# A sparse graph transformer on one core: ranks inverted by one-hot products on TensorE, lists gathered per tile, first attention from the eighth query tile

## The chip, the cores and the metric

The kernel runs on one core of a Trainium2 chip. Its engines are named as in the profile: PE (TensorE, matrix products), DVE (VectorE), ACT (ScalarE), POOL (GpSimd) and SP, which only issues transfers. The metric is the device time of one execution in microseconds; the runs of the kernel before took 1945.95, 1947.1 and 1948.37 us, so the median is 1947.1 us.

## The reference

Two layers of a graph transformer over 2708 tokens of 512 features, with 8 heads of 64. A token attends only to the tokens that `adj` joins it with (itself included); the adjacency is sparse.

```python
mask = adj.astype(jnp.float32) + jnp.eye(n, dtype=jnp.float32)
q = (h @ Wq.T + bq).reshape(n, N_HEADS, D_K)
k = (h @ Wk.T + bk).reshape(n, N_HEADS, D_K)
v = (h @ Wv.T + bv).reshape(n, N_HEADS, D_K)
scores = jnp.einsum('nhd,mhd->hnm', q, k) / jnp.sqrt(jnp.float32(D_K))
scores = jnp.where(mask[None, :, :] == 0, jnp.float32(-1000000000.0), scores)
attn = jax.nn.softmax(scores, axis=-1)
ctx = jnp.einsum('hnm,mhd->nhd', attn, v).reshape(n, D_MODEL)
attn_out = ctx @ Wo.T + bo
h1 = _layer_norm(h + attn_out, ln1_g, ln1_b)
ff = jax.nn.relu(h1 @ W1.T + b1) @ W2.T + b2
h2 = _layer_norm(h1 + ff, ln2_g, ln2_b)
```

The second layer does the same with the first layer's output and its own weights. All is float32; the hidden layer of the feed-forward has 2048 columns.

## The kernel before

**Tiles.** The 2708 tokens are 22 tiles (NT) of 128, the last with 20 tokens. Keys and values of a layer are written to memory as one row of 1024 numbers per token (kv_d), queries as rows of 512 (q_d). Attention never forms the full score matrix: for each token there is a list of at most 24 neighbours, and rows of kv_d are gathered by list position, 128 tokens at a time, by indirect transfers that POOL issues.

**Ranks.** Tokens have between 1 and 22 neighbours. They are put in order of that count, longest list first, and attention works on tiles of ranked tokens. Tile g then needs only `CAPS[g]` gathers: 22 for tile 0, 7 for tiles 16 to 18, 6 for tile 19, 5 for tile 20. The work goes in blocks of two ranked tiles: (20, 19), (18, 17), (7, 9), (6, 10) and so on; `order` is that list laid flat.

**Stage 1, `first` (0 to about 157 us).** For each of 22 tiles PE makes k and v; DVE adds the bias to k (L879), ACT copies v (L881) and writes the pair to kv_d. Beside it `lists` turns rows of `adj` into lists: POOL adds the diagonal, ACT makes codes of position and flag (L681), DVE takes the greatest by groups of eight (L684 to L691). With the last tile `counted` finds each token's count, the place of each count in the order (`before`, `hot`), and the records `rec`: 24 list entries, the token's own number in column 24, and padding to 32 numbers (128 bytes).

**Stage 2, `first_queries` (about 162 to 285 us).** For each of 22 tiles PE makes q; DVE scales it and adds the bias (L929); SP writes pairs of tiles to q_d. At t = 1 `ranked` makes each token's rank (two PE products, L763 and L770, and four DVE operations), and POOL scatters the 22 tiles of records to their rank in `rec_d` (L789), then loads them back in ranked order in three parts (L801, L808); the token numbers go to `ident_i`, the lists to `idx`, and a penalty for unused places to `minus` (`listed`). `own_rows` gathers the x rows of the first ranked tiles, `own_query` makes their queries directly, since q_d isn't complete yet. At t = OWN (13) those of tiles 20 and 19 are made and attention begins; at each later t `advance` lets attention emit more of its steps.

**Attention, `attend`.** The lists are cut into chunks of at most two gathered rows per token (1024 or 2048 numbers a partition). A chunk's steps are the product with the query (L1055) and its sum by head (L1061) on DVE; one step later the exponentials (L1074) and the weighting (L1081) on ACT and the sums on DVE (L1087, L1094); two steps later, for a tile's last chunk, the tile's sums and the reciprocal (L1102 to L1117); three steps later ACT's division to `cx` (L1125). `advance(c)` adds c to a credit, at most 1.5, and emits steps while it is positive and fewer than two tiles are done and not taken. A chunk of two rows costs 1. Gathers are issued three chunks ahead (EARLY), into five buffers (KVB).

**After attention.** `attended` transposes cx on PE (L1191), multiplies by Wo (o, L576), adds x, and norms on DVE with a power on POOL (L1181). `feed_forward` makes 16 slices f of the hidden layer (pf, L1383; ACT's relu to ft, L1394) and, three slices later, the second product (a, L1356). During the feed-forward of one block attention for the next is emitted; `through(k+1)` at f = 10 (11 for the first block) makes it complete.

**What sets the order.** PE, ACT and SP take the order of the source (`manual_schedule`). POOL does so in stages 1 and 2 and in layer 0's feed-forward, DVE in `first_queries`; elsewhere a scheduler orders DVE and POOL, and it moves an independent DVE operation into the gap between two dependent ones. An engine runs its instructions strictly in the built order, so one that waits holds all that stand behind it. Buffers come from pools: q takes turns in three PSUM banks "g" (even t) and three "f" (odd t), and k, v, transposes and own queries share them.

Of the kernel before, what the change touches and what calls it, by code (L numbers as in the profile page):

```python
# [43 lines left out]
XB, XBS = 256, 11  # L44
LEAD = 1.3
QT = 6
OWN = 13
EARLY = 3
FIRST = 5
PACE = (0.62, 0.72)  # L50


# [420 lines left out]
def by_edges(ctx: ExitStack, tc: tile.TileContext, x, xT, adj, layers, out, good):  # L473
# [130 lines left out]
    def lists_of(pa):  # L604
# [7 lines left out]
        for code in codes:  # L612
# [13 lines left out]
        nc.gpsimd.memset(top[:, NT - 1, :], 0.0)  # L626
        rec = pa.tile([P, NT, 32], F32, tag="rec", name="rec", bufs=1)
        nc.gpsimd.memset(rec, 0.0)
        nc.gpsimd.iota(
            rec[:, :, LIST : LIST + 1],  # L630
            [[P, NT], [1, 1]],
            base=0,
            channel_multiplier=1,
            allow_small_or_imprecise_dtypes=True,
        )
        by = pa.tile([P, LIST], F32, tag="by", name="by", bufs=1)
        nc.gpsimd.iota(
            by,
# [15 lines left out]
        new = dn.tile([P, NC, 2 * P], F32, tag="hT", name="new", bufs=1)  # L654
        new = new.rearrange("p c t -> p (c t)")[:, : NT * 32]
        new = new.rearrange("p (g c) -> p g c", c=32)
        nc.gpsimd.memset(new, 0.0)
        nc.gpsimd.dma_start(
            out=rec_d[: (NT - 1) * P, :].rearrange("(g p) c -> p g c", p=P),
            in_=new[:, : NT - 1, :],  # L660
        )
        nc.gpsimd.dma_start(out=rec_d[(NT - 1) * P :, :], in_=new[:LW, NT - 1, :])

        full = []

# [90 lines left out]
        def ranked(hot, before, half):  # L756

            at = pa.tile([P, NT], F32, tag="at", name="at", bufs=1)
            for h in range(2):
                ts = slice(h * half, (h + 1) * half)  # L760
                pr = ps_a.tile([P, DM], F32, tag=f"a{h}", name="pr")
                w = half * LIST
                nc.tensor.matmul(  # L763
                    pr[:, :w],
                    tri,
                    hot[:, ts, :].rearrange("p t e -> p (t e)"),
                    start=True,
                    stop=False,
                )
                nc.tensor.matmul(  # L770
                    pr[:, :w],
                    ones,
                    before[:, ts, :].rearrange("p t e -> p (t e)"),
                    start=False,
                    stop=True,
                )
                nc.vector.tensor_tensor(
                    hot[:, ts, :].rearrange("p t e -> p (t e)"),
                    hot[:, ts, :].rearrange("p t e -> p (t e)"),
                    pr[:, :w],  # L780
                    ALU.mult,
                )
                nc.vector.tensor_reduce(at[:, ts], hot[:, ts, :], AX.X, ALU.add)
            ranks = pa.tile([P, NT], I32, tag="ranks", name="ranks", bufs=1)
            nc.vector.tensor_copy(ranks, at)
            moved = []
            for t in range(NT):
                r = size(t)
                move = nc.gpsimd.indirect_dma_start(  # L789
                    out=rec_d[:, :],  # L790
                    out_offset=bass.IndirectOffsetOnAxis(ap=ranks[:r, t : t + 1], axis=0),
                    in_=rec[:r, t, :],
                    in_offset=None,
                    bounds_check=N - 1,
                    oob_is_err=False,
                )
                tc.declare_no_dep(move.ins, group="moved", reason="no two tokens have one rank")
                tc.add_to_no_dep_group("moved", move.ins)
                moved.append(move)
            def back(a, b):  # L800
                load = nc.gpsimd.dma_start(  # L801
                    out=new[:, a:b, :],
                    in_=rec_d[a * P : b * P, :].rearrange("(g p) c -> p g c", p=P),
                )
                return load

            first, last = NT - FIRST, NT - 1
            rest = nc.gpsimd.dma_start(out=new[:LW, last, :], in_=rec_d[last * P :, :])  # L808
            for load in (rest, back(first, last), back(0, first)):
                for move in moved:  # L810
                    tc.add_manual_dep(
                        load.ins,
                        move.ins.name,
                        mybir.DependencyInfo(
                            mybir.DependencyClass.Sync, mybir.DependencyReason.DATA
                        ),
                        reason="every list is in its place",
                    )
            nc.gpsimd.tensor_copy(ident_i[:, first:], new[:, first:, LIST])

        def listed(start):

            ts = slice(NT - FIRST, NT) if start else slice(0, NT - FIRST)
            if not start:
                nc.gpsimd.tensor_copy(ident_i[:, ts], new[:, ts, LIST])
            some = new[:, ts, :LIST]
            nc.vector.tensor_scalar(idx[:, ts, :], some, 1.0, 1.0, ALU.max, ALU.subtract)
            nc.vector.tensor_scalar(minus[:, ts, :], some, 0.0, NEG, ALU.is_equal, ALU.mult)

        return lists, counted, ranked, listed  # L830

    def first(w, meanwhile):

# [33 lines left out]
        bk = next(turning)  # L867
        wv = matrix(w, "Wv", "wv")
        pa = tc.tile_pool(name="pa", bufs=2)
        lists, counted, ranked, listed = lists_of(pa.__enter__())  # L870
        done, before = 0, None
        for t in range(NT):
            r = size(t)
            xs = tokens(t, 0)
            kv = wts.tile([P, 2 * DM], F32, tag=f"w2_{5 + t % 3}", name="kvs")
            k = project(xs, r, wk, "k")
# [4 lines left out]
            nc.scalar.copy(kv[:r, DM:], v[:r])  # L881
            if before:
                nc.scalar.dma_start(**before)
            if t == NT - 1:
                counts = counted()
            plus_rest(kv[:r, :DM], k, r)
            plus_rest(kv[:r, DM:], v, r)
            before = dict(out=kv_d[0][t * P : t * P + r, :], in_=kv[:r])
# [9 lines left out]
                bq = next(turning)  # L898
                finish(turning)
        nc.scalar.dma_start(**before)  # L900
        return bq, wq, counts, ranked, listed, pa, tokens

    def first_queries(bq, wq, counts, ranked, listed, pa, tokens, meanwhile):

        nonlocal at
        made = []

        def written():
# [9 lines left out]
        for t in range(NT):  # L918
# [2 lines left out]
                written()  # L921
            q = project(tokens(t, 1), r, wq, "q", other=t % 2 > 0)
            if t == 1:
                ranked(*counts)
                xrs = [own_rows(g) for g in order[:3]]
            if t % 2 == 0:
                qs = wts.tile([P, 2, DM], F32, tag=f"w2_{5 + t // 2 % 3}", name="qs")
                made.append((t, qs))
            nc.vector.scalar_tensor_tensor(  # L929
                qs[:r, t % 2], q[:r], DK**-0.5, bq[:r], ALU.mult, ALU.add  # L930
            )
            plus_rest(qs[:r, t % 2], q, r, DK**-0.5)
            if t == OWN - 1:
                listed(True)
                pa.__exit__(None, None, None)
                at = ctx.enter_context(tc.tile_pool(name="at", bufs=2))
                for g in order[:3]:
# [6 lines left out]
                    own_query(g, zT, to[g], bq, wq)  # L944
                    advance(0.5)
            if t == OWN + 1:
                listed(False)
                xr = own_rows(order[3])
            if t == OWN + 4:
                own_query(order[2], zTs[2], to[order[2]], bq, wq)  # L950
                zT = turned_own(order[3], xr)
            meanwhile(t)
            if t == NT - 1:
                g = order[3]
                own[g] = at.tile([P, DM], F32, tag="q", name="q", bufs=QB)
                own_query(g, zT, own[g], bq, wq)
# [584 lines left out]
    def beside_queries(t):  # L1541
# [5 lines left out]
            now.load_w1(len(now.w1), nc.scalar)  # L1547
            now.load_w2(len(now.w2), nc.scalar)
        if t > OWN:
            advance(1.0 if t < NT - 3 else 0.6)  # L1550
        if t == NT - 3:
            through(0)
            early[0] = now.attended(blocks[0], got)
            next(early[0])
        if t == NT - 2:
            for _ in blocks[0]:
                next(early[0])

# [176 lines left out]
```

## Time and profile before

| what | value |
| --- | --- |
| median of three runs | 1947.1 us |
| the profiled execution | 1944.02 us, its span 1942.3 us |
| mean granted clock of PE | 0.982 |
| DMA in the span | 366.92 MB, 189 GB/s on average |
| PE busy, 100 to 150 us / 200 to 250 us | 48.52 / 47.46 us |
| PE busy, 350 to 400 us / 900 to 1000 us | 45.74 / 100.00 us |

A line of a timeline has the start in us from the span's start, the duration in us, the engine, the source line, the operation, the tile written and those read, shapes, the count of merged instructions, and in brackets the idle time before it with what ended it. A PE product of float32 counts twice: its 4 parts stand as x8.

The gathers of keys are the costliest group of POOL, and the key products of DVE:

```profile
L1018 POOL DMA_INDIRECT kv<-kv_d,idx x420 | 544.5, 1296 | 461.8 <-DVE acc L1094 272.4
L1055 DVE TENSOR_TENSOR kv<-kv,q 128x1024 f32<-128x1024 f32 (+3 forms) x222 | 254.3, 1157 | 171.1 <-DMA kv<-kv_d,idx 139.9
```

After the bar stand busy time and the mean of one in ns, then the idle time before such an instruction and what ended most of it.

### The profile page before, as it was taken

The numbers are of one execution on the slowest core, as the hardware profiler recorded it, in microseconds if no ns is written. First come the engines' busy times: TensorE is split into PE (matmuls) and PEld (weight loads), VectorE is DVE, ScalarE is ACT, GpSimd is POOL, SyncE is SP. The second block draws the span as 40 slices with busy tenths as digits, with TensorE's granted clock in tenths as the row PEclk, the third lists the DMA queues.
The fourth block names the chain that finished last, engine by engine and source line by source line (L and its number), as shares of the span: only waits on it lengthen the run. The fifth ranks groups of instructions, "written<-read, shape, count | busy, mean of one in ns | idle before, by whom it ended". The sixth has DMA issues, their size and how long they took to land.

```text
span 1942.3 us, 20878 instructions
## 1 busy us (share of the span) xinstructions
PE 1859.4 (96%) x6162; PEld 1098.8 (57%) x6162; DVE 1321.4 (68%) x2172; ACT 934.0 (48%) x3219; POOL 804.6 (41%) x710
## 2 busy tenths in 40 slices
PE   8998968999999999999999997999999999999997
PEld 4443426556666565665666553566666665666664
DVE  5885467758658686785840337697977998878422
ACT  4560135545536555474452113556465766655511
POOL 3013525435536555463510114354555776546101
PEclk9999978999999999999999999999999999999999
DMA  9998747556645665554501368665665766544000
GB/s 330 345 319 297 260 151 269 181 176 198 199 159 181 215 201 175 188 185 151 170 17 65 110 237 325 215 220 186 216 213 165 262 215 235 184 154 151 17 1 19
DMA packets 131486, 366.92 MB, mean 189 GB/s; under 512 B 16669, under 2 KB 37005, under 8 KB 128655
## 3 DMA queue, kind: packets, MB, share of 16 engines
q0 software_dynamic: 69120, 246.35, 38.0%
q1 hardware_dynamic: 53332, 99.66, 14.9%
q10 hardware_dynamic: 8910, 19.48, 2.7%
q8 instruction: 50, 0.82, 0.2%
q14 instruction: 74, 0.60, 0.1%
HBM read 314.62 MB, written 50.83 MB: 188 GB/s over the span
## 4 chain that ended last, share of the span: by engine, by line
PE 48%; issue 3%; DVE 3%; DMA 1%; POOL 1%; ACT 1%; POOLq 0%; SPq 0%; DVEq 0%
PE pf L1383 19%; PE a L1356 18%; PE o L576 4%; PE q L576 2%; PE k L576 1%; PE v L576 1%; PE tp L1191 1%; DVE kv L1055 1%; POOL kv L1018 1%; DVE sc L1061 1%; DMA kv<-kv_d,idx 1%; PE a L1371 1%; DMA q<-q_d 0%; DVE acc L1094 0%; POOL rd L1181 0%
## 5 line engine op out<-in xcount | busy, mean ns | idle before, releaser
L1018 POOL DMA_INDIRECT kv<-kv_d,idx x420 | 544.5, 1296 | 461.8 <-DVE acc L1094 272.4
L1383 PE MATMUL pf<-hT,w 128*128 128x256 f32 (+1 forms) x2816 | 637.2, 374 | 6.7 <-ACT ft L1394 5.2
L1383 PEld LDWEIGHTS pf<-hT,w 128*128 128x128 f32 x2816 | 521.4, 192 | 181.8 <-issue 104.1
L1356 PE MATMUL a<-w,ft 128*128 128x512 f32 x1312 | 615.0, 595 | 6.1 <-ACT ft L1394 3.6
L1055 DVE TENSOR_TENSOR kv<-kv,q 128x1024 f32<-128x1024 f32 (+3 forms) x222 | 254.3, 1157 | 171.1 <-DMA kv<-kv_d,idx 139.9
L1394 ACT ACTIVATE ft<-pf,b 128x256 f32<-128x256 f32 (+1 forms) x336 | 153.8, 463 | 432.7 <-PE pf L1383 428.8
L1356 PEld LDWEIGHTS a<-w,ft 128*128 128x128 f32 x1312 | 247.8, 191 | 196.5 <-issue 169.3
L1081 ACT ACTIVATE kv<-kv,p 128x64 f32<-128x64 f32 x1232 | 311.0, 334 | 5.0
L1061 DVE TENSOR_REDUCE sc<-kv 128x16 f32<-128x1024 f32 (+3 forms) x222 | 253.7, 1152 | 1.5
L1094 DVE TENSOR_TENSOR acc<-acc,kv 128x1024 f32<-128x1024 f32 (+2 forms) x178 | 203.9, 1145 | 17.5 <-ACT kv L1081 15.5
L1181 POOL TENSOR_TENSOR rd<-va,mhalf 128x1 f32<-128x1 f32 (+1 forms) x88 | 90.0, 1023 | 273.5 <-DVE va L1179 271.9
L576 PE MATMUL o<-wo,cT 128*128 128x512 f32 x336 | 149.7, 598 | 0.5 <-ACT cT L1196 0.5
L1087 DVE TENSOR_TENSOR kv<-kv,p 128x512 f32<-128x512 f32 (+1 forms) x178 | 121.2, 681 | 36.1 <-ACT p L1074 36.1
L1074 ACT ACTIVATE p<-sc,minus 128x8 f32<-128x8 f32 x420 | 102.8, 294 | 72.0 <-DVE sc L1061 43.6
L1125 ACT ACTIVATE cx<-acc,su 128x64 f32<-128x64 f32 (+1 forms) x352 | 88.5, 334 | 71.1 <-DVE su L1117 54.2
L576 PEld LDWEIGHTS o<-wo,cT 128*128 128x128 f32 x336 | 64.1, 192 | 82.3 <-issue 72.1
L681 ACT ACTIVATE code<-aj 128x2708 bf16<-128x2708 int32 (+1 forms) x22 | 73.2, 3328 | 50.2 <-POOL aj L677 41.7
L684 DVE MAX8 tops<-code 128x8 f32<-128x247 f32 (+2 forms) x242 | 83.1, 401 | 20.1 <-ACT code L681 20.1
L1185 DVE SCALAR_TENSOR_TENSOR h<-h,rd,ln_b 128x512 f32<-128x512 f32 (+1 forms) x88 | 65.6, 746 | 41.1 <-POOL rd L1181 41.1
L1081 ACT ACTIVATE acc<-kv,p 128x64 f32<-128x64 f32 (+1 forms) x352 | 88.8, 335 | 1.4
L1443 ACT COPY kvs<-v 128x512 f32<-128x512 f32 (+1 forms) x22 | 12.9, 585 | 158.8 <-PE v L576 138.4
L1415 DVE TENSOR_TENSOR h<-a,h 128x512 f32<-128x512 f32 (+1 forms) x44 | 29.8, 678 | 83.3 <-PE a L1356 44.5
(159 smaller groups left out, 1586.8 us busy)
## 6 DMA issues: line engine op xcount, KB each, us to landing
aj<-in_adj SPq DMA_DIRECT2D x21, 1354.0 KB
kv_d<-kvs ACTq DMA_DIRECT2D x21, 512.0 KB
w<-in_W SPq DMA_DIRECT2D x20, 512.0 KB
xg<-in_xT SPq DMA_DIRECT2D x19, 512.0 KB
kv<-kv_d,idx POOLq DMA_INDIRECT x420
w<-in_W ACTq DMA_DIRECT2D x12, 512.0 KB
q_d<-qs SPq DMA_DIRECT2D x22, 256.0 KB
zT_d<-zT SPq DMA_DIRECT2D x22, 256.0 KB
```

The costliest lines, as they stand in the source:

```text
L576: nc.tensor.matmul(o[:r], xs(c), wm[:, c, :], start=(c == 0), stop=(c == NC - 1))
L1018: return nc.gpsimd.indirect_dma_start(out=to, out_offset=None, in_=table[:, :], in_offset=bass.IndirectOffsetOnAxis(ap=s, axis=0), bounds_ ...
L1055: nc.vector.tensor_tensor(kv[:r, :c, :DM], kv[:r, :c, :DM], self.q[:r].unsqueeze(1).to_broadcast([r, c, DM]), ALU.mult,)
L1061: nc.vector.tensor_reduce(self.sc[:r, s0 : s0 + c, :], kv[:r, :c, :DM].rearrange("p s (h d) -> p s h d", d=DK), AX.X, ALU.add,)
L1074: nc.scalar.activation(p[:r, s, :], self.sc[:r, s, :], AF.Exp, bias=minus[:r, g, s : s + 1])
L1081: nc.scalar.activation(to[:, i, hd], kv[:r, i, DM + h * DK : DM + (h + 1) * DK], AF.Copy, scale=p[:r, s0 + i, h : h + 1],)
L1087: nc.vector.tensor_tensor(to[:, 0, :].rearrange("p (h d) -> p h d", d=DK), kv[:r, 0, DM:].rearrange("p (h d) -> p h d", d=DK), p[:r, s0, : ...
L1094: nc.vector.tensor_tensor(self.acc[:r, :c, :], self.acc[:r, :c, :], kv[:r, :c, DM:], ALU.add)
L1181: nc.gpsimd.tensor_tensor(rd[:r], va[:r], mhalf[:r], ALU.pow)
L1356: nc.tensor.matmul(a[:r], fts[f][:, c0 : c0 + r], self.w2[f // 2][:, f % 2, :], start=(f == 0), stop=(f == NFC - 1),)
L1383: nc.tensor.matmul(pf[:, :w], self.w1[f // 2][:, c, f % 2 * P : f % 2 * P + P], hT[:, c, :w], start=(c == 0), stop=(c == NC - 1),)
L1394: nc.scalar.activation(ft[:, :w], pf[:, :w], AF.Relu, bias=self.b1[:, f : f + 1])
```

## The change

Seven things are changed.

1. `rec` no longer holds the token's number, and `rec_d` isn't filled with zeros at the start. POOL makes three counting tables instead: `token`, `starts`, `lanes`.
2. `ranked` doesn't scatter. ACT issues a plain write of the records to `rec_d` in token order; DVE splits each rank into its tile and its place in it, and makes one-hot tables: `one` (place) and `who` (tile, times the token's number).
3. `inverted`, called at t = 4, multiplies the tables on PE, 22 products of 128x128 by 128x22 in one PSUM bank: the result is `ident_i`, the token at each rank.
4. `fetched` gathers the records of one ranked tile by `ident_i`: four tiles at t = 4, the other 18 two per t from t = 8. `listed` converts them in four parts, at t = 6, 17 and 21.
5. OWN goes from 13 to 7: own queries are made at t = 7, and attention is advanced by 0.65 a tile from t = 8 instead of 1.0 (0.6 at the end) from t = 14. The attention of block 0 is completed and taken at t = 18 instead of 19, o follows at t = 19 instead of 20, and the own query of tile 17 comes at t = 20 instead of 21.
6. DVE takes the order of the source from t = 20 of `first` on, and `counted` stands ahead of the last tile's products.
7. The query tiles take turns in their three buffers from the second one on, not the first.

```diff
-OWN = 13
+OWN = 7
...
+        token = counting("token", [P, NT], [[P, NT]], 1)
+        starts = counting("starts", [P, NT], [[P, NT]], 0)
+        lanes = counting("lanes", [P, P], [[1, P]], 0)
...
-        nc.gpsimd.memset(new, 0.0)
-        nc.gpsimd.dma_start(
-            out=rec_d[: (NT - 1) * P, :].rearrange("(g p) c -> p g c", p=P),
-            in_=new[:, : NT - 1, :],
-        )
...
+        nc.gpsimd.memset(new[:, NT - 1, :], 0.0)
...
-            for t in range(NT):
-                r = size(t)
-                move = nc.gpsimd.indirect_dma_start(
-                    out=rec_d[:, :],
-                    out_offset=bass.IndirectOffsetOnAxis(ap=ranks[:r, t : t + 1], axis=0),
-                    in_=rec[:r, t, :],
...
+            nc.scalar.dma_start(
+                out=rec_d[: (NT - 1) * P, :].rearrange("(g p) c -> p g c", p=P),
+                in_=rec[:, : NT - 1, :],
+            )
+            nc.scalar.dma_start(out=rec_d[(NT - 1) * P :, :], in_=rec[:LW, NT - 1, :])
...
+            nc.vector.tensor_copy(whole, at)
+            nc.vector.tensor_scalar(whole, whole, P - 1, None, ALU.bitwise_and)
+            nc.vector.tensor_copy(lane, whole)
+            nc.vector.tensor_tensor(at, at, lane, ALU.subtract)
+            parts = []
+            for h in range(2):
+                ts = slice(h * half, (h + 1) * half)
+                table = pa.tile([P, N], F32, tag=f"code{h}", name="table", bufs=1)
+                wide = half * P
+                one = table[:, :wide].rearrange("p (t c) -> p t c", c=P)
+                who = table[:, wide : wide + half * NT].rearrange("p (t g) -> p t g", g=NT)
+                nc.vector.tensor_tensor(
+                    who,
+                    at[:, ts].unsqueeze(2).to_broadcast([P, half, NT]),
+                    starts.unsqueeze(1).to_broadcast([P, half, NT]),
+                    ALU.is_equal,
+                )
+                nc.vector.tensor_tensor(
+                    who, who, token[:, ts].unsqueeze(2).to_broadcast([P, half, NT]), ALU.mult
+                )
+                nc.vector.tensor_tensor(
+                    one,
+                    lane[:, ts].unsqueeze(2).to_broadcast([P, half, P]),
+                    lanes.unsqueeze(1).to_broadcast([P, half, P]),
+                    ALU.is_equal,
+                )
+                parts.append((one, who))
+            return parts
+
+        def inverted(parts):
+
+            to = ps_a.tile([P, DM], F32, tag="a0", name="to")
+            t = 0
+            for one, who in parts:
+                for i in range(NT // 2):
+                    r = size(t)
+                    nc.tensor.matmul(
+                        to[:, :NT],
+                        one[:r, i, :],
+                        who[:r, i, :],
...
+            nc.vector.tensor_copy(ident_i, to[:, :NT])
+
+        def fetched(tiles):
+
+            for g in tiles:
+                r = size(g)
+                gather(new[:r, g, :], rec_d, ident_i[:r, g : g + 1])
+
+        def listed(a, b):
+
+            some = new[:, a:b, :LIST]
...
+            if t == NT - 2:
+                in_turn.enter_context(tc.manual_schedule(engines={mybir.EngineType.DVE}))
+            if t == NT - 1:
+                counts = counted()
...
             if t == 1:
-                ranked(*counts)
+                parts = ranked(*counts)
+            if t == 4:
+                inverted(parts)
+                fetched(order[:4])
                 xrs = [own_rows(g) for g in order[:3]]
             if t % 2 == 0:
-                qs = wts.tile([P, 2, DM], F32, tag=f"w2_{5 + t // 2 % 3}", name="qs")
+                qs = wts.tile([P, 2, DM], F32, tag=f"w2_{5 + (t // 2 + 1) % 3}", name="qs")
...
             if t == OWN - 1:
-                listed(True)
+                listed(NT - 5, NT - 1)
...
+            if OWN < t and later:
+                fetched(later[:2])
+                del later[:2]
+            if t == NT - 5:
+                listed(5, 12)
+            if t == NT - 1:
+                for a, b in ((0, 5), (12, NT - 5), (NT - 1, NT)):
+                    listed(a, b)
...
-            if t == NT - 1:
+            if t == NT - 2:
                 g = order[3]
...
         if t > OWN:
-            advance(1.0 if t < NT - 3 else 0.6)
-        if t == NT - 3:
+            advance(0.65)
+        if t == NT - 4:
             through(0)
             early[0] = now.attended(blocks[0], got)
             next(early[0])
-        if t == NT - 2:
+        if t == NT - 3:
             for _ in blocks[0]:
                 next(early[0])
```

## The prediction

> **What bounds the kernel now.** I read the page's engine totals first, then the busy time by stage, then the waits of PE, then the timelines of PE, DVE and POOL in the stage that the change touches.
>
> ```profile
> PE 1859.4 (96%) x6162; PEld 1098.8 (57%) x6162; DVE 1321.4 (68%) x2172; ACT 934.0 (48%) x3219; POOL 804.6 (41%) x710
> PEclk9999978999999999999999999999999999999999
> ```
>
> PE is busy for 96% of the span. So only time in which PE stands still, or runs at a lower granted clock, can be won; one slice, the sixth (243 to 291 us), has the lowest clock.
>
> ```profile
> 150.00:200.00 50.00, 44.87 (x117) 19.93 (x116) 24.65 (x67) 1.39 (x3) 19.23 (x21) 0.97 0.85 288
> 250.00:300.00 50.00, 31.93 (x92) 17.37 (x92) 31.84 (x47) 17.46 (x69) 10.19 (x10) 0.76 0.39 130
> 300.00:350.00 50.00, 44.84 (x141) 27.51 (x140) 37.21 (x50) 27.30 (x106) 27.68 (x22) 0.93 0.81 284
> ```
>
> These are stretches of 50 us with the busy time of PE first, the clock third from the end. From 250 to 300 us PE works 31.9 of 50 us, at clock 0.76. It is the end of the query pass and the start of the first feed-forward. The timeline of PE says where (start, time, instruction, idle time before it and its releaser):
>
> ```profile
> 161.84 8.83 PE L576 MATMUL q<-wq,xg 128*128 128x512 f32 x16 [5.13 <-DVE kvs L879]
> ...
> 265.15 1.91 PE L1191 MATMUL tp<-ident,cx 128*128 128x128 f32 x4 [13.87 <-ACT cx L1125]
> 266.86 5.71 PE L576 MATMUL q<-wq,xg 128*128 128x512 f32 x8
> ...
> 288.44 1.11 PE L1191 MATMUL tp<-ident,h 128*128 128x128 f32 x4 [3.66 <-DVE h L1185]
> 290.01 9.62 PE L1383 MATMUL pf<-hT,w 128*128 128x256 f32 x32 [0.46 <-ACT hT L1196]
> ```
>
> 5.13 us are lost before the first query, 13.87 us for the attention of tile 19 (cx), 3.66 us for the normed rows; 2.53 us more for the gathered rows xr (215 to 218 us). Together with 0.46 that is 25.65 us. The work between the last value product (ends 156.7) and the feed-forward (290.0) is, at full pace, 99.9 us: 21 query tiles and 4 own ones of 3.43, the odd tile 0.9, four rank products 1.8, transposes 3.4, o 6.87, the hT copy 1.1. It took 133.3, so 33.4 are lost: 25.65 of idle time and 7.8 of slow matmuls after it (the tile at 266.86 took 5.5 instead of 3.43 us to the next start).
>
> Why cx came late is in DVE's and POOL's timelines:
>
> ```profile
> 255.24 1.22 DVE L1055 TENSOR_TENSOR kv<-kv,q 128x1024 f32<-128x1024 f32 x1 [4.35 <-DMA kv<-kv_d,idx]
> ...
> 262.23 0.69 DVE L1055 TENSOR_TENSOR kv<-kv,q 128x512 f32<-128x512 f32 x1 [1.16 <-DMA kv<-kv_d,idx]
> ...
> 264.29 0.19 DVE L1117 RECIPROCAL su<-su 128x8 f32<-128x8 f32 x1
> ```
> ```profile
> 175.16 1.11 POOL L789 DMA_INDIRECT rec_d<-rec,ranks  x1 [23.96 <-DVE ranks L785]
> ...
> 202.17 0.91 POOL L789 DMA_INDIRECT rec_d<-rec,ranks  x1 [0.30 <-issue]
> ...
> 212.60 0.99 POOL L1018 DMA_INDIRECT kv<-kv_d,idx  x1 [0.30 <-issue]
> ...
> 261.33 0.99 POOL L1018 DMA_INDIRECT kv<-kv_d,idx  x1 [2.46 <-DVE acc L1094]
> ```
>
> POOL scatters 22 lists, 1.27 us apart, before the first gather of keys at 212.6. DVE then meets two key products that stand, in the built order, ahead of tile 19's reciprocal but belong to tile 18; both wait for gathers that were queued late.
>
> **What the Trainium skill says.** "TensorE: Matmul & The Clock Gate", section "What's actually happening": an idle window of about 3.4 us puts PE at half clock. The trace agrees: the clock is 0.50 from 255 to 270 us, after the 13.87 us wait. So a wait that goes takes a slow stretch with it. The same page, section "LDWEIGHTS (loading the stationary operand)": columns / 1.2 GHz, 107 ns for 128 columns. The trace's four transposes take 0.43 us from start to start, 0.108 each: it agrees. "DMA: Bandwidth & Descriptors", section "Specifications": transfers under 512 B become read-modify-write. List rows are 128 B, but the trace shows no backlog of them: POOL waits only 1.6 us after its last scatter.
>
> **The change part by part.**
>
> (1) DVE order around the counting. Three key biases now stand before `counted`, so the bank of the first query is free when DVE ends the top lists at 152.5: 152.5 + 3 x 0.6 = 154.4, and PE is done with v at 156.7. The 5.13 us wait goes, and with it the slow first queries (8.66 us from start to start instead of 6.87): +6.9. The counting itself ends near 163 (8.3 us of small rows), so the rank products at 163.6 find it ready. Tile w2_6 instead of w2_5 for the first queries takes away a 5.1 us wait of DVE for the last kv write; PE didn't feel it, the ranks do.
>
> (2) Inversion. DVE: five small operations (0.9) and, twice, two of 242 elements (0.4 each) and one of 1408 (1.63, by 1.22 for 1024 and 0.68 for 512): 5.8 us, done near 176.0. PE reaches `to` after q4 at 175.7. 22 f32 products are two passes each; 44 x 0.108 = 4.8 us. Bounds: 2.2, if a 22-column pass costs half, 8.4, if the 191 ns busy time of a weight load counts whole. I take 4.8 and 0.3 of waiting: -5.1.
>
> (3) Lists. `to` ends near 180.7; four list gathers (1.3 us each, by the scatter and key gather rows) and three xr follow, to 190.1. PE has q5 to q7, to 191.1, and waits for xr as before (5 to 6 us from issue to use): 0 change. First keys are asked for at 190.1 instead of 212.6. Issue of the direct write of the lists is on ACT, idle then; the zero fill and the three loads back go.
>
> (4) POOL in the query stage. From 190 to 240 it now issues 18 list gathers (23.4 us) between the key gathers. I walked its queue: 7 keys to 199.2, xr 200.5, then pairs of lists and pairs of keys, each key pair released by DVE before its turn, to 229.1; six or seven lists to 236.9; two xb to 239.5; then the single key of tile 18's last chunk, issued by 240.5, landed by 243.5. That product again stands ahead of tile 19's reciprocal on DVE. So reciprocal 244, cx 246; PE asks for it at 244.4. The old 13.87 becomes about 2, and 2 of slow clock where 3.4 to 4 were: +13.5 net. Bounds of the new wait: 0 (keys land in 2 us and DVE frees buffers early) to 8 (landing takes 5 and POOL slips a pair).
>
> DVE has room for it: from own query 0 (199.7) to 244 it has 11 query evacuations, 2 own ones, six chunks of 4.35 and sums, 38 of 44 us; the pace of 0.65 instead of 1.0 chunk a tile is what keeps PE's 3.43 us per tile free of DVE. On SP the write of the first query pair, and the x load of tiles 6 and 7 behind it, go about 1 us later (DVE's tables stand before query 1's evacuation, near 176.6): landed by 184, when PE reaches q6; I cost it at nothing, at most 2.
>
> (5) h. Attention is finished a tile earlier in the loop, and o stands before a query tile and an own one, 7 us more of PE work ahead of the transposes of h. DVE has 4.2 us per normed tile: h of tile 19 near 264.5, PE there at 265. The 3.66 goes, the hT copy stays: +4.1. I leave 0.5 of its slow clock out.
>
> Sum to the feed-forward's start: 6.9 - 5.1 + 13.5 + 4.1 = 19.4; with the slow stretches around 215 to 230 and before 290 that no longer have a cause (2), 21.5: it starts near 268.5, not 290.0.
>
> (6) Feed-forward of block 0. It took 77.3 us (290.0 to 367.3) where 63.7 is full pace. Some seven chunks of two keys must still pass DVE, 4.35 us each (two of 1.22 for the scores, 0.68 and 1.22 for the sums); after the change DVE has 5 us more left at its start (a key product, the odd query rows 2.1, list conversions 1.6), but fewer waits for keys and no slow first pass. ft sits behind attention on ACT: I find stalls near f6 and f9 of about 5 each. That is what it loses now. I take 0; bounds -6 to +8. Block 1's 6 us of waits: +1. After `through(1)` the emission is in the same state as before, so later blocks and layer 1 move along unchanged.
>
> Total about 22.5. Against the profiled execution's 1944.0 us (span 1942.3) this gives 1921.5; the median of the runs shown, 1947.1, is 3.1 higher, so 1924.5.
>
> **Rivals.**
> A. The gain is larger: attention starts 22 us earlier, so DVE also catches up and the stalls of feed-forward 0 go (13.6), with block 1's: 22.5 + 16 = 1908. For it: DVE waits about 9 us for keys and p in that stage. Against: step 6's backlog.
> B. DVE's backlog decides: feed-forward 0 stalls by 6 to 10 more and the new cx wait is 6: gain 10, 1937. For it: ACT holds ft behind cx, and cx(18) behind DVE.
> C. Slower: POOL's queue becomes the bound. All 18 list gathers stand before tile 18's last key; if one costs not 1.3 but about 2.8 us (they share eight completion lanes, and each waits for the one eight earlier), that key is issued 27 us later, near 268, and DVE, cx, PE wait for it with half clock after: the loss passes the 22 won. At 3.2 us each it is 1955. For it: in the trace a q_d write issued at 180.07 beside the scatters was used only at 205.7. Against: POOL kept 1.27 us through all 22, and the scatters landed 1.6 us after the last.
> D. The inversion on PE and the kept xr wait eat what the rest brings: 1946, no change.
>
> **How the numbers follow.** Forecast (gain 15 to 30) 0.54, A 0.17, B 0.15, D 0.05, C 0.09. About 0.2%, 3.9 us, is what a measurement here can tell from no change. So faster 0.86, same 0.05, slower 0.09. The predicted time is the forecast's, 1924. Its own range is 1916 to 1932; to leave out no more than two in ten the range takes in most of A and B: 1906 to 1940.
>
> **What would show it.** Right: no wait before the first query; `to` near 176; first keys gathered near 190; cx wait of PE under 8 us; feed-forward from about 268. Wrong: PE waits longer than 5 us at `to` (step 2); list gathers further apart than 1.3 us, or a DVE key product waiting over 8 us near 236 (step 4); feed-forward 0 far from 77 us (step 6); a difference after 450 us (the claim that later stages only move).

## The result, and the profile after

The changed kernel takes 1959.9 us in the median of five runs (1957.96 to 1965.42), the kernel before 1947.1 us (1945.39 to 1948.37): a ratio of 1.0070, with a 95% interval of 1.0053 to 1.0087. It is slower by 0.7% where 1924 us were forecast. The profiled execution has a span of 1958.1 us against 1942.3 us. That difference, 15.8 us, is larger than the one between the medians, 12.8, because the kernel before was profiled in one of its quicker executions.

What the change set out to do in the query stage did happen. This is PE's timeline of the changed kernel, in the form explained above:

```profile
155.65 4.56 PE L575 MATMUL q<-wq,xg 128*128 128x512 f32 x10
...
174.70 5.09 PE L829 MATMUL to<-table 128*128 128x22 f32 x44
...
253.16 1.23 PE L1228 MATMUL tp<-ident,cx 128*128 128x128 f32 x4 [9.43 <-DVE qs L959]
254.18 5.85 PE L575 MATMUL q<-wq,xg 128*128 128x512 f32 x8
...
288.88 1.65 PE L1420 MATMUL pf<-hT,w 128*128 128x256 f32 x3 [12.77 <-ACT hT L1233]
```

The first query starts at 155.65 us without a wait; it was 161.84 after a wait of 5.13. The inversion runs at 174.7 without a wait. But two waits stand further on: 9.43 us ahead of the transposes of cx (13.87 before), with a slow tile after it as before (5.7 us to the next start, where 3.43 is full pace), and a new one of 12.77 us ahead of the first feed-forward product, where it was 0.46. So the feed-forward starts at 288.9 us instead of 290.0: of 21.5 us forecast, 1.1 came.

Who held hT is seen on ACT and DVE. The first fence is ACT's timeline of the changed kernel, the second DVE's:

```profile
287.42 2.18 ACT L1233 ACTIVATE hT<-tp,b 128x128 f32<-128x128 f32 x8 [19.27 <-issue]
```
```profile
251.00 0.69 DVE L1092 TENSOR_TENSOR kv<-kv,q 128x512 f32<-128x512 f32 x1 [15.81 <-DMA kv<-kv_d,idx]
251.61 0.20 DVE L1154 RECIPROCAL su<-su 128x8 f32<-128x8 f32 x1
...
287.18 0.16 DVE L849 TENSOR_SCALAR minus<-new 128x24 f32<-128x24 f32 x1
287.26 1.20 DVE L1098 TENSOR_REDUCE sc<-kv 128x16 f32<-128x1024 f32 x1
```

The transposes of h are on PE at 274.7 us, yet ACT copies hT only at 287.42, 0.1 us after DVE's last read of `new` ends (287.18 + 0.16). The trace names no releaser for ACT ("issue"); that it is this buffer is tested below. `new`, the gathered lists, is made with the tag hT (L661) and lies in the one buffer that hT needs. In the kernel before its last read started at 230.9 us, as the view of the tile `new` shows (count, shortest, median and longest in ns, first and last start):

```profile
L828 DVE TENSOR_SCALAR minus<-new x2: 268/418/568, 211.0 to 230.9; 128x120 f32<-128x120 f32 x1, 128x408 f32<-128x408 f32 x1
```

Now it is the conversion of the last lists (the last three of five calls of `listed`, at t = 21), behind the query tiles and key products that DVE still had to do.

The wait for cx is the one forecast, but longer. POOL's timeline of the changed kernel:

```profile
191.74 1.00 POOL L1055 DMA_INDIRECT kv<-kv_d,idx  x1 [2.38 <-DMA q_d<-qs]
...
241.51 0.96 POOL L1055 DMA_INDIRECT new<-rec_d,ident_i  x1 [0.30 <-issue]
242.77 1.04 POOL L1055 DMA_INDIRECT xb<-in_x,ident_i  x1 [0.30 <-issue]
244.12 1.00 POOL L1055 DMA_INDIRECT xb<-in_x,ident_i  x1 [0.30 <-issue]
245.43 1.00 POOL L1055 DMA_INDIRECT kv<-kv_d,idx  x1 [0.30 <-issue]
```

The first keys are asked for at 191.74 us instead of 212.6, and a list costs the 1.3 us that was reckoned. But tile 18's last key is asked for at 245.43 and used at 251.00; DVE stands still for it 15.81 us, with tile 19's reciprocal behind. Behind it stands also the query bias (qs, L959) that PE's line names: the transposes need a PSUM bank that a query tile still held. ACT began cx at 251.84, so both things that PE needed came out of this one wait of DVE.

From there on the time was to move along unchanged, and it did not. The table sets the forecast beside what the first pf of each feed-forward block shows (change against the kernel before, profiled executions, us):

| stretch | forecast | measured |
| --- | --- | --- |
| start of the first feed-forward block | -21.5 | -1.1 |
| first block (77.3 before, 80.2 after) | 0 | +2.9 |
| second block (85.9, 82.2) | -1 | -3.7 |
| third block (78.3, 82.4) | 0 | +4.1 |
| fourth to sixth block | 0 | -1.9 |
| seventh block (80.1, 84.1) | 0 | +4.0 |
| second block of the second layer (70.8, 76.2) | 0 | +5.4 |
| all others, to PE's last product | 0 | -0.9 |
| after POOL's last transfer (7.2, 14.2) | 0 | +7.0 |
| span | -22.5 | +15.8 |

In the last row but one no engine computes. The view of one source line (the last line of the program) shows it; columns are the engine's sequencer, the count, shortest, median and longest in ns, and the first and last start. Before, and then after:

```profile
L1731 POOLq DRAIN  x3: 46/107/2683, 1938.8 to 1942.0; - x3
```
```profile
L1768 POOLq DRAIN  x3: 46/107/8318, 1948.9 to 1957.8; - x3
```

POOL's last drain takes 8.32 us instead of 2.68, and the step ahead of it on POOL's sequencer (INC_SWDGE_SEM in the trace) 2.22 us instead of 0.84. The other engines take their next step only at 1957.4 us, when the drain has ended.

### The profile page after: what moved, and what is told of

It reads as the page before. It is cut to its first block, busy times and chain, and to the rows that moved or that the text cites. A ratio compares the mean times of both kernels' runs of the same rounds, so it can differ in the third digit from the quotient of the medians.

```text
span 1958.1 us, 20966 instructions
## 1 busy us (share of the span) xinstructions
PE 1866.8 (95%) x6206; PEld 1104.6 (56%) x6206; DVE 1327.6 (68%) x2188; ACT 931.8 (48%) x3219; POOL 806.0 (41%) x705
## 4 chain that ended last, share of the span: by engine, by line
PE 40%; DVE 8%; issue 5%; DMA 3%; POOL 2%; ACT 1%; SPq 0%; POOLq 0%; DVEq 0%
PE pf L1420 16%; PE a L1393 16%; PE o L575 4%; DMA kv<-kv_d,idx 2%; DVE kv L1092 2%; DVE sc L1098 1%; PE k L575 1%; PE v L575 1%; PE tp L1228 1%; POOL kv L1055 1%; DVE acc L1131 1%; DVE kv L1124 1%; DMA q<-q_d 1%; POOL rd L1218 1%; PE q L575 1%
```

## The experiments

Each kernel was timed beside the kernel before on the same chip; the ratio is to that, with its 95% interval. Where a run is compared with the changed kernel, the ratio to the kernel before is the common measure (1.0070 for the changed kernel).

**A buffer of its own.** Is it the shared buffer that holds hT?

```diff
-        new = dn.tile([P, NC, 2 * P], F32, tag="hT", name="new", bufs=1)
+        new = wts.tile([P, NC, DM], F32, tag="wk", name="new")
```

(made where the inversion starts, when Wk is no longer used)

> Only edit to the changed kernel: the gathered lists have a buffer of their own (the idle place of Wk) instead of the one that hT also uses. Theory S (shared buffer): hT no longer waits for the last list conversions; the copy runs about 1 us after the transposes of h (274.7), PE's first pf starts near 276.5 instead of 288.9 with a wait of 1 to 2 us instead of 12.77, the block after it starts about as much earlier, and the end is about 12 us earlier, 1945 to 1949. Rival B (backlog): the feed-forward starts near 276.5 but DVE and ACT have the same attention work left, so that the third block starts where it did (451 us, within 4) and the time stays 1955 to 1961. Rival O (order on ACT): hT waits for its turn on ACT, so the first pf stays at 288 to 289 and the time at 1958 to 1961.

Measured: 1944.3 us (12 runs), ratio 0.9988 (0.9973 to 1.0002). PE's timeline of this kernel:

```profile
274.85 1.43 PE L1230 MATMUL tp<-ident,h 128*128 128x128 f32 x8
277.00 5.45 PE L1422 MATMUL pf<-hT,w 128*128 128x256 f32 x24 [0.71 <-ACT hT L1235]
```

The wait is 0.71 us, the first pf at 277.0, the third block at 436.5 instead of 451.3. The shared buffer is the cause; rival O falls, and rival B too, since the third block gained even more than the first. From 1.0070 to 0.9988 is 0.8% of the time, more than the changed kernel loses to the kernel before.

**The lists out of the keys' way, twice.** First the late ones behind the query loop:

```diff
-            if OWN < t and later:
+            if OWN < t and len(later) > 11:
                 fetched(later[:2])
                 del later[:2]
...
         all_made.append(True)
+        fetched(later)
```

(their conversion goes to the seventh slice of the first feed-forward block)

> As the kernel with a buffer of its own for the lists, and only 7 of the 18 interleaved lists are gathered during the queries; the other 11 are gathered after the query loop and converted in the first feed-forward block. Theory P (POOL's queue): the last key gather of tile 18 is issued some 11 x 1.3 = 14 us earlier, near 231 instead of 245.4; the product that waits for it no longer holds tile 19's reciprocal up, PE's wait of 9.43 us for cx falls under 3, the first pf starts 8 to 14 us earlier than with the own buffer alone, near 265, and the time is 1936 to 1944. Rival K: that gather is held by the key buffers that DVE and ACT free, not by the lists: it is issued at 240 or later, the cx wait stays 6 to 10 and the time is that of the own buffer within 3 us. Rival B: the first pf comes earlier, the third block does not, and the time stays within 4 us of the own buffer's.

Taken by pairs, 8 lists stayed beside the keys and 10 were late. Measured: 1943.9 us (20 runs), ratio 0.9975 (0.9962 to 0.9988). The key is used at 239.5 us instead of 251.0, no wait for cx is left, and the first pf starts at 266.1. So the queue was what held the key, as theory P says, and rival K falls. But the time is that of the own buffer: the first block takes 85.0 us and the third starts at 435.6. Rival B's numbers came, for a reason that is not backlog, as the trace has it and two later kernels test. DVE's timeline of this kernel, and then POOL's:

```profile
291.88 1.23 DVE L1093 TENSOR_TENSOR kv<-kv,q 128x1024 f32<-128x1024 f32 x1 [10.71 <-DMA kv<-kv_d,idx]
```
```profile
283.51 0.96 POOL L1056 DMA_INDIRECT new<-rec_d,ident_i  x1 [0.30 <-issue]
284.77 1.04 POOL L1056 DMA_INDIRECT kv<-kv_d,idx  x1 [0.30 <-DMA new<-rec_d,ident_i]
```

The ten lists stood ahead of the next keys again, only of others. POOL was idle from 238 to 258 us, so that was the next place to try, with the lists emitted at t = NT - 3:

> Own buffer for the lists, 7 lists gathered beside the keys as before, the other 11 in POOL's idle time behind tile 18's last key gather (238 to 258 us, where POOL waits for the norm) instead of ahead of the keys (the changed kernel) or behind the query loop (the kernel with late lists, where DVE then waited 10.71 us for keys at 291.9). Theory: the first pf starts near 266 as with the late lists, the first feed-forward block takes 76 to 80 us instead of 85.0, the third block starts at 424 to 430 instead of 435.6, and the time is 1934 to 1940. Rival B (backlog): DVE and ACT have the same attention left to do, the first block stays at 83 or more, the third block starts at 433 to 438 and the time is 1942 to 1946.

Measured: 1944.0 us (20 runs), ratio 0.9987 (0.9975 to 0.9999); first pf at 274.8, third block at 434.1. The theory's start did not come, because the lists landed one place too early. POOL's timeline of this kernel, and then PE's:

```profile
243.01 0.96 POOL L1059 DMA_INDIRECT new<-rec_d,ident_i  x1 [0.30 <-issue]
244.28 1.04 POOL L1059 DMA_INDIRECT kv<-kv_d,idx  x1 [0.30 <-issue]
```
```profile
251.12 1.09 PE L1232 MATMUL tp<-ident,cx 128*128 128x128 f32 x4 [8.48 <-DVE qs L961]
```

The wait for cx is back, and the first pf is 8.7 us later than with the lists behind the loop. Rival B has the time and the third block right, but not the first block: it took 78.5 us, not 83.

**Parts of the change alone.** The kernel before with only the counting ahead of the last key bias and the query buffers turned by one:

```diff
+            if t == NT - 2:
+                in_turn.enter_context(tc.manual_schedule(engines={mybir.EngineType.DVE}))
+            if t == NT - 1:
+                counts = counted()
...
-                qs = wts.tile([P, 2, DM], F32, tag=f"w2_{5 + t // 2 % 3}", name="qs")
+                qs = wts.tile([P, 2, DM], F32, tag=f"w2_{5 + (t // 2 + 1) % 3}", name="qs")
```

> The kernel before with the first part of the change alone: the counting stands before the last key bias in VectorE's written order, and the query buffers turn by one. Theory: the 5.13 us wait and the slow stretch behind it go, the first query starts at about 156 instead of 161.8, everything after it, the scatters too, moves 5 to 7 us earlier, and the time is 1940 to 1943. Rival: PE's waits further on (xr, cx 13.87) take it back, because they hang on POOL's scatters; then these waits grow by as much and the time is 1945 to 1948.

Measured: 1934.7 us (6 runs), ratio 0.9932 (0.9912 to 0.9953). The first query starts at 156.5 us without a wait. The part is worth having: 13 us by the medians, 9 to 17 by the interval, more than the 4 to 7 that the theory had. The profiled execution, the slowest of the six, shows only 3.3 of them: a new wait of 4.64 us for xg follows at 184, and the first pf is 3.2 us earlier. Where the others win the rest, no trace shows.

Then the changed kernel with the attention where it was before (`OWN = 13`, `advance(1.0)`, the block taken in one tile later), lists gathered at t = 5 to 13:

> The changed kernel with the attention put back to where it stood before (14th query, 1.0 chunk a tile, the block taken in one tile later); the lists are gathered in pairs beside queries 5 to 13, when POOL has nothing else. Theory: what is lost in the changed kernel is lost by the lists between the keys and by the shared buffer at the end; here the lists are out of the way, but their last conversions still stand at the end, so hT waits for them as long as the attention is late; the first pf is at 283 to 292 and the time 1945 to 1955. Rival: the time stays near 1960, so the moved attention was not where it was lost. Second rival: under 1943, so that the inversion alone was worth having and the move spoiled it.

Measured: 1947.1 us (12 runs), ratio 1.0004 (0.9991 to 1.0018); first pf at 288.2 after waits of 12.72 us for cx and 4.02 for hT. The first theory's range holds. So the inversion without the moved attention gains nothing in this form. It even costs something, for this kernel has the first part in it too, which alone gave 13 us. By the traces about half of that is the long end (14.0 us after POOL's last transfer), which it shares with every kernel that leaves the two plain writes of the lists on ACT's queue; the kernel before with its first part alone has the short one (7.3).

**The end of the program.** The kernel with the lists in the gap was run with five lists gathered twice, with the two plain writes of the lists on POOL's queue instead of ACT's, and with fifteen lists gathered twice:

```diff
                 fetched(later)
+                fetched(order[:5])
```
```diff
-            nc.scalar.dma_start(
+            nc.gpsimd.dma_start(
                 out=rec_d[: (NT - 1) * P, :].rearrange("(g p) c -> p g c", p=P),
```

> As the kernel with the lists in POOL's gap, and five lists are gathered a second time in the same gap, so that POOL issues 535 transfers in all, as many as the kernel before, instead of 530. This tests the end of the program: in the changed kernel and all that are made from it POOL's last two sequencer steps (levelling its transfers' semaphores, and a drain) take 2.2 and 8.3 us, in the kernel before 0.8 and 2.7. Theory N (number): what is left to clear at the end depends on how many transfers POOL has issued; with 535 the two steps take 0.8 and 2.7 and the time falls by 7 us under that of the kernel with the lists in the gap. Rival D (direct transfers): it depends on the five plain transfers that the kernel before has on POOL and the changed one has not; then they stay 2.2 and 8.3, and the time is unchanged within 2 us.

Measured: 1947.9 us (12 runs), ratio 1.0007 (0.9994 to 1.0020). The drain is 8.73 us and the step ahead of it 2.31. Theory N falls: five more gathers made it 0.41 us longer. The time rose by 3.9 us, where rival D allowed 2; in the traces the first pf is where it was and later blocks are longer, for no known reason.

> As the kernel with the lists in POOL's gap, but the two plain writes of the lists to memory are issued on POOL's queue instead of ACT's, 532 transfers of POOL in all. Rival D (direct transfers on POOL decide the length of the last drain): the last two steps of POOL take about 0.8 and 2.7 us. Theory N (their number decides): they take 2.2 and 8.3, or another length that fits 532 but not the kind. The start of the first pf stays within 2 us of 266.

Measured, one run: 1936.5 us, below all twenty runs of the kernel that it is made from (1938.7 to 1951.9); the drain 1.05 us, the step ahead of it 0.44, shorter even than the 2.7 and 0.8 of rival D; first pf at 273.2, not near the 266 expected but near the 274.8 of its parent.

> As the kernel with the lists in the gap, and 15 lists are gathered a second time (545 transfers of POOL). The drain was 8.32 us at 530, 8.73 at 535, 1.05 with two plain writes of 2708 rows more, 2.68 in the kernel before (535, five of them plain). Theory M (leftover of a ring): 0.082 us a gather makes 8.32 us 101 gathers' worth; a plain pass over 2708 rows is 21 gathers' worth; 122 left 13 and 143 left 33, so about 109 are cleared at a time, and 116 should leave 7: a drain near 0.6 us and a levelling step of 0.3 to 0.5. Rival D (plain transfers shorten it): the drain goes on growing, to 9.5, and the levelling to 2.4 or more.

Measured, one run: 1965.4 us; the drain is 9.54 us, the step 2.52. Theory M falls, rival D's line holds (0.082 us for each gather more). The first pf went to 286.7 in this kernel: the next keys were asked for only at 269.3, behind all 25 lists, and DVE waited 19.76 us for them with the norm behind, so its time says nothing of the end.

Then the two writes on POOL's queue as the only edit to the changed kernel:

> The changed kernel with one edit: the two plain writes of the lists are issued on POOL's queue instead of ACT's. Theory: only the end changes, POOL's last two steps go from 2.2 + 8.3 to 0.4 + 1.05 us, the first pf stays at 287 to 290, and the time falls by 7 to 10 us, to 1950 to 1953. Rival: the end is shorter but the writes hold POOL or the lists up, or the end wasn't on the path: 1956 or more.

Measured: 1954.2 us (4 runs, 1947.6 to 1959.0), ratio 1.0061 (1.0039 to 1.0082). The trace is clear; the view of the program's last line in this kernel:

```profile
L1768 POOLq DRAIN  x3: 46/107/1050, 1943.9 to 1945.5; - x3
```

From POOL's last transfer to the end are 5.2 us instead of 14.2, and the first pf is at 289.3. The median fell by 5.7 us, between theory and rival, and the two intervals of the ratio overlap: these runs alone do not show what the shorter end is worth.

**The later blocks.** In the changed kernel the third block is 4.1 us longer, though the source emits the same work in it. POOL's timelines there, before and then after:

```profile
470.97 1.00 POOL L1018 DMA_INDIRECT kv<-kv_d,idx  x1 [0.30 <-issue]
481.69 1.01 POOL L1018 DMA_INDIRECT q<-q_d,ident_i  x1 [9.72 <-DVE kv L1055]
485.26 2.05 POOL L981 DMA_INDIRECT kv_d<-kvs,ident_i  x1 [2.55 <-ACT cx L1125]
487.61 1.01 POOL L1018 DMA_INDIRECT kv<-kv_d,idx  x1 [0.30 <-issue]
488.93 1.00 POOL L1018 DMA_INDIRECT kv<-kv_d,idx  x1 [0.30 <-issue]
```
```profile
473.50 1.20 POOL L1055 DMA_INDIRECT kv<-kv_d,idx  x1 [0.30 <-issue]
484.57 2.04 POOL L1018 DMA_INDIRECT kv_d<-kvs,ident_i  x1 [9.87 <-issue]
486.92 1.03 POOL L1055 DMA_INDIRECT kv<-kv_d,idx  x1 [0.30 <-issue]
492.36 1.01 POOL L1055 DMA_INDIRECT q<-q_d,ident_i  x1 [4.41 <-DVE kv L1092]
```

Before, the gather of a tile's last key row (470.97) and that of the next query stood ahead of the write of the next layer's keys (kv_d<-kvs). After the change that key row (486.92) stands behind this write, and the next query and its keys behind the key row. DVE waits 11.49 us for these keys, at 504.6; counted from the block's first pf, that product starts after 53.2 us instead of 50.0. The cause to test: once the queries are done, a sixth key buffer (the place of Wq) takes turns with the five others. In the kernel before the 17th chunk is the first to get it, in the changed one the 18th, since one chunk more has been asked for by then. One of the five others is lent to the values that kv_d's write reads, so it now falls to another chunk to wait for that write.

```diff
-            places.extend([None] * KVB + ["wq"])
+            places.extend([None] * (KVB - 1) + ["wq", None])
```

> The changed kernel with one edit: the sixth key buffer (the place of Wq) enters the rotation of the key buffers one chunk earlier, at the 17th chunk, where it stood in the kernel before; in the changed kernel it is the 18th, because one more chunk has been asked for when the queries end. From the second feed-forward block on POOL and DVE then have the order of the kernel before, in which no last key row overtakes a pair and no pair waits behind the write of the next layer's keys. Theory R (rotation): the third block takes 78 to 80 us instead of 82.4, the seventh 80 to 81 instead of 84.1, the second block of the second layer 71 to 73 instead of 76.2; the first pf stays at 288 to 290; the time falls by 8 to 12 us, to 1948 to 1953. Rival T (timing): these blocks are longer because of when the attention stands against them, not of its order; they stay at 82, 84 and 76 within 1 us, and the time stays 1957 to 1962.

Measured: 1946.2 us (13 runs), ratio 0.9996 (0.9983 to 1.0009), below the theory's 1948. The third block takes 78.3 us, the seventh 79.9: rotation, not timing. The second layer's second block takes 74.4, outside both forecasts; what makes it vary was not found. POOL's timeline of this kernel has the old order again:

```profile
475.55 1.01 POOL L1055 DMA_INDIRECT q<-q_d,ident_i  x1 [8.13 <-DVE kv L1092]
479.11 2.03 POOL L1018 DMA_INDIRECT kv_d<-kvs,ident_i  x1 [2.56 <-issue]
481.45 1.03 POOL L1055 DMA_INDIRECT kv<-kv_d,idx  x1 [0.31 <-issue]
```

The first pf is at 286.1, after the same 12.77 us for hT: 2.8 us earlier than in the changed kernel, which the edit does not explain.

**All together.** Own buffer, writes on POOL, and the late lists one place further back, behind tile 18's keys and ahead of the norm's powers:

```diff
+            if t == NT - 3:
+                waiting.append(lambda: fetched(later))
...
         if t == NT - 3:
+            waiting.pop()()
             for _ in blocks[0]:
                 next(early[0])
```

> Own buffer, list writes on POOL's queue, and the late lists moved one place back on POOL: behind tile 18's last key gather and ahead of the norm's two powers. (In the kernel with the lists in the gap they stood ahead of that gather, and PE waited 8.48 us for cx.) Theory: the cx wait goes, the first pf starts at 263 to 267 instead of 273.2, the first feed-forward block is 76 to 80 us, so that the third block starts at 424 to 430, and with the short end the time is 1926 to 1932. Rival B (backlog of the attention on DVE, ACT and POOL): the first block or the second gets longer by what the start gains, the third block starts at 433 to 437, and the time is 1934 to 1940.

Measured: 1929.2 us (6 runs), ratio 0.9929 (0.9908 to 0.9949). First pf at 266.8, no wait for cx, first block 78.0, third block at 426.7. The theory holds, rival B falls. Against the kernel with the writes on POOL and the lists ahead of the keys (first pf at 273.2) the new place alone makes 6.4 us of the start. With the buffers' turn as well:

> Own buffer for the lists, their late ones behind tile 18's keys, the plain writes on POOL's queue, and the rotation of the key buffers as in the kernel before. Theory R: against the kernel without the rotation's edit (1929.2 us) the third, the seventh and the second block of the second layer get 3 to 5 us shorter each, first pf still at 265 to 268, and the time is 1915 to 1922. Rival T: 1926 to 1932, the blocks as they were (83.2, 84.3, 74.8).

Measured: 1917.8 us (5 runs, 1914.8 to 1924.8), ratio 0.9854 (0.9828 to 0.9880). First pf at 265.2, third block 79.4, seventh 80.3. The second layer's second block takes 73.6, only 1.2 us less, where theory R had 3 to 5; the rest of the theory holds. PE's timeline of this kernel where the changed one lost 12.77 us:

```profile
265.15 5.45 PE L1425 MATMUL pf<-hT,w 128*128 128x256 f32 x24 [0.71 <-ACT hT L1238]
```

It beats both kernels: the change, with four small edits, gives 30 us where it cost 13. Of these 30 the change's first part gave 13 in its own runs.

## Why the prediction was wrong

Step (1), DVE's order around the counting: right in the changed kernel, to the 5.13 us. Alone it was confirmed as a gain.

Step (2), the inversion: right for the products. PE was there at 174.7 (175.7 forecast) and took 5.09 us (4.8), without the 0.3 of waiting. What follows them was put at nothing: PE's granted clock was 0.50 to 0.69 from 180 to 184 us, with no idle time before, and the next query tile took 5.4 us to the next start, without its wait for xg, instead of 3.43.

Step (3), lists: right, but for the wait for xr, which was to stay. First keys were asked for at 191.74 (190.1); that wait was gone, and one of 1.16 us for xg stood ahead of the seventh query instead (step (4) allowed at most 2 for it).

Step (4), POOL's queue: the mechanism was right, the size was not. "Issued by 240.5, landed by 243.5" was 245.43 and 251.00; the wait for cx "about 2", bounded by 8, measured 9.43, with the slow tile behind it as before. The queue was 5 us longer than walked, and the row took 5.6 us from issue to use, not 3. The sign given for this came: a key product of DVE waited 15.81 us, where over 8 was named. The rival that took the queue for the bound (C) had the direction right by luck: it priced a list at 2.8 us or more, and it cost 1.30. Only its order, all lists ahead of tile 18's last key, is what the runs bore out.

Step (5) failed, and it is the largest miss: "The 3.66 goes, the hT copy stays". The 3.66 did go, but the step looked only at what hT reads. hT also writes a buffer, and the last list conversions, moved to the end of the loop, still read it. The own buffer showed this wait to be 12.77 us at its place and 15.6 us of the median. The wait for hT (12.3 us above the forecast) and that for cx (7.4 above) make up 19.7 of the 20.4 us by which the first feed-forward started later than forecast.

Step (6) failed in its last sentence: "After `through(1)` the emission is in the same state as before, so later blocks and layer 1 move along unchanged". The emission was, but not the turn of the key buffers. That cost 8 us in two blocks and went away with one edit; the 5.4 us of the second layer's second block stay open. The stalls of the first block did move within the bounds given (+2.9 of -6 to +8).

The sum had no term for what follows the last transfer. It was 7.0 us in the profiled executions.

The earlier start that the prediction reckoned with can be had: with these obstacles out of the way the first pf is at 265.2 us, 3.3 us better than step (5) had it.

## What to carry to other kernels

When work is moved, list for every tile that it reads and writes whose buffer it is and who needs that buffer next; a shared tag turns a harmless late read into a wait of another stage. Ask also what else counts along: a rotation that starts "when this is done" starts elsewhere when the work before it moves. And put optional transfers of an in-order queue behind the transfer that someone waits for, checking the built place: ten short gathers one place too early cost 6.4 us of start, and behind the loop they held the keys of the next stage instead.

## What the runs showed of the hardware

The end of a program can depend on the transfers that POOL has issued long before. With 530, 535 and 545 gathers the last drain took 8.32, 8.73 and 9.54 us, 0.082 us for each more; with two plain writes of 2708 rows in all on the same queue at the start of the query stage it took 1.05 us, in all four kernels that have them there. Whether it is their kind, their size or their place that shortens the drain is open: the kernel before has five plain transfers on that queue, and its drain takes 2.68 us.

PE's granted clock can fall without idle time. In all twelve kernels with the inversion it went from 1.00 to 0.50 during its 44 products of 22 columns or just behind them, for some 3 to 7 us, though PE had no wait of more than 0.21 us ahead of it since its first query; the kernel before has 1.00 throughout, from 166 to 188 us. The query tile behind took 5.0 to 6.2 us to the next start, waits left out, instead of 3.43. Where the clock fell within the products they took up to 6.88 us instead of 5.09. No run varies the width of the products, so that it is the narrowness which does it is not shown.

"Perfetto Trace Analysis" of the Trainium skill, section "DMA Instruction — SWDGE (GPSIMD)", says that such a transfer's slice ends when its descriptors are made, not when its data have moved. The trace agrees: the gather at 245.43 us is busy for 1.00 us, and the product that waits for it starts at 251.00.
